# Expert masks by DMA instead of by transpose, two alternating PSUM pairs in the mixed expert blocks, and the second feed-forward beside the first

## The chip, the cores and the metric

The kernel runs on one core of one Trainium2 chip. The metric is the device time of one launch in microseconds, as the median of several runs. A profiled execution gives the trace; its span is the time from the first to the last instruction of the program.

Engine names in the profile: PE is TensorE's matmul, PEld its weight load, DVE is VectorE, ACT is ScalarE, POOL is GpSimd, SP is the queue from which most transfers are issued.

## The reference

One transformer layer in float32 on 4 x 1024 tokens of width 256: a linear-attention block with a feed-forward, and a mixture of experts with low-rank adapters, each inside `x + layernorm(f(layernorm(x)))`. Cut to what matters here:

```python
# attention part, per token block
h = h @ ...                                   # q, k, v, linear attention, wo
x = x + gelu(layernorm(x) @ w_ff1 + b_ff1) @ w_ff2 + b_ff2
x = x @ w_d + b_d

# expert part: D = 256, F = 1024, E = 8 experts, rank R = 16, top K = 2
t = rmsnorm(x) * norm_w
probs = softmax(t @ gate_w.T)
topw, topi = top_k(probs, 2); topw = topw / topw.sum()
base1, base3 = t @ w1.T, t @ w3.T
h1[e] = base1 + 2 * (t @ a1[e].T) @ b1[e].T
h3[e] = base3 + 2 * (t @ a3[e].T) @ b3[e].T
act[e] = silu(h1[e]) * h3[e]
out[e] = act[e] @ w2.T + 2 * (act[e] @ a2[e].T) @ b2[e].T
out = sum over the two chosen experts of weight * out[e]
```

The 8 experts of rank 16 fill 128 partitions together. So the adapters of all experts are one matmul with 128 rows, and a mask of 128 partitions by 512 tokens, 2 where the partition's expert is the token's and 0 elsewhere, keeps the token's own 16 rows.

## The kernel before

**Stages.** The 4096 tokens are eight blocks of 512 (`BLK`), four tiles of 128 (`TB`). `front(i)` makes queries, keys and the context, `middle(i)` the attention's output and the feed-forward in two halves of 256 tokens (`hf`), and `tail(i, hf)` the routing: it sorts each token by its pair of experts and scatters its row of 263 values (`RW`: 256 of x, then the lower and the higher expert `R_LO`, `R_HI`, the weight `R_W`, and others) into the DRAM tensor `rows`. The experts are numbered so that each is in a lower or an upper half (64 partitions each). `ORDER` lists eight expert blocks of 512 rows: four `LU` (one expert in each half; "mixed" below), three `H` (both experts in one half), one `G` (any pair). For each, `prepare(n, ...)` loads the rows and makes masks, weights and the masked adapter inputs, and `experts(n, kind)` does the main work. A branch at the end repeats everything with G blocks when a group has too few places; with this data it isn't taken.

**Order of the work.** The order on TensorE, VectorE, ScalarE and GpSimd is written out by a planner while the program is built. Each stage is a generator wrapped in a `Stream`; a number that it yields is the time at which it wants to go on, a function is a condition. `now()` counts the planned TensorE time; `V`, `A` and `G` book a cost on VectorE, ScalarE and GpSimd; `defer` puts GpSimd work into a list that `catch_up` empties. In the loop at L1578, `side()` picks the first stream of `sides()` that can go on, in the order closing, `prepare_q`, `prepare` (`ready`), tails, fronts, middles (`blocks`) and the rest. Only where no side work can go does the main stream (`experts`) step, and after it a filler from `finals`, the output matmuls of a block. Each engine, and SP too, then works strictly in the order that came out. SP carries the loads of x and z, the stores `kept`, and the loads of `row`.

**prepare, L1011.** L1014 loads the rows (526 KB, in H two loads of 263 KB), three planned microseconds ahead of their use. VectorE compares the expert numbers of a tile with `eidx` (0 to 7, sixteen times each, along the free dimension) into `sel` (L1025 for LU, L1035 for H, L1042 and L1079 for G), which gives the mask with tokens on partitions. `flip` (L299) transposes it on TensorE, four 128x128 tiles to a PSUM tile `pm`, and ScalarE copies it out, times 2, as `m0` (L1057). `weights()` (L1060) does the same for the weight, broadcast over 128 columns: four transposes into `pmw`, then copies into `wt` (L1064) and, by kind, `m1` (L1066 for LU, L1069 and L1070 for H). LU calls it ahead of the token transposes, H and G at the end of `prepare`. There `dm`, the difference of two masks, has been kept in the tile of `wt`. `normed` and `transposed` make the tokens `tT`, and the matmuls `pu` with the adapter inputs times the masks give `u0`.

**LU in experts, L1431 on.** For each of eight f (128 of the 1024 hidden features): `base` makes `ph`, two PSUM banks (for w1 and w3) of one fixed pair `banks(mine)`; ScalarE copies both into the banks `py` (L1449); `halved` adds the low half's adapter to `ph` and the high half's to `py` by matmuls with 64 rows, and applies tanh (L1233) and two VectorE steps each (L1236, L1237); `down_lu` multiplies by `a2`; `mixed` lets GpSimd blend the two activations. `output` (L1333) is the filler: `up` multiplies the blended values by `w2` into the other pair, four matmuls for each f, as soon as GpSimd is through; `finish` adds `b2`. The next LU block may begin its f 0 and f 4 only when the block before has that many of these done (L1442).

**H and G.** `whole_base` alternates the pairs from f to f; `inner` adds the adapters and calls `swiglu` (L1173, L1175, L1176) once for each of the two experts; `rest` (L1378) makes the outputs at the end of a block.

**middle, L755.** L787 lets a block go on to its feed-forward only when that of the block before is through (`fed`); `x1T`, `h2T` and the hidden tiles `g` have one set of buffers.

Of the kernel before, what the change touches and what calls it, by code (L numbers as in the profile page):

```python
# [15 lines left out]
P = 128  # L16
# [37 lines left out]
def sandwich_kernel(  # L54
# [42 lines left out]


# [10 lines left out]
    eidx_b = eidx_f.unsqueeze(1).to_broadcast([P, TB, P])  # L109
    eidx_h = eidx_f.rearrange("p (h r) -> p h r", h=2)  # L110
# [339 lines left out]
    a2_s = wp.tile([P, FC, P], F32, tag="a2_s", name="a2_s")  # L450

    def prepare_ranks():

        yield lambda: once.done
        raw = mp1.tile([P, DC, 2 * P], F32, tag="actB", name="a13_raw")
# [299 lines left out]
    def middle(i):  # L755
# [31 lines left out]
        yield lambda: i == 0 or i - 1 in fed  # L787

        x1T = mp1.tile([P, DC, BLK], F32, tag="copy", name=f"x1T_{i}")
        h2T = blk([P, DC, BLK], "h2T", f"h2T_{i}")  # L790
# [17 lines left out]
        for hf in range(2):  # L808
            ts = slice(hf * W, (hf + 1) * W)
            gs = []  # L810
            for fp in range(FC // 2):
                pf = psum(f"pf_{i}_{hf}_{fp}")
                g = gp.tile([P, BLK], F32, tag="g", name=f"g_{i}_{hf}_{fp}")
# [16 lines left out]
                yield 0.0  # L830
            yield end

            sty, mvy = tiles(f"y_{i}_{hf}", HT)
            for j in range(hf * HT, (hf + 1) * HT):
# [12 lines left out]
                if j % HT < HT - 1:  # L847
                    yield 0.0
# [162 lines left out]
    def prepare(n, kind, src):  # L1011
        row = sp.tile([P, TB, RW], F32, tag="row", name=f"row_{n}")
        for t, ap in src:
            nc.sync.dma_start(out=row[:, t, :], in_=ap)  # L1014
        yield now() + 3.0
        yield lambda: ranked.done
# [4 lines left out]
        sel = m1.rearrange("p (t r) -> p t r", r=P)  # L1021
        if kind == "LU":

            for j in range(TB):
                nc.vector.tensor_tensor(  # L1025
                    sel[:, j, :].rearrange("p (h r) -> p h r", h=2), eidx_h,
                    row[:, j, R_LO : R_HI + 1].unsqueeze(2).to_broadcast([P, 2, HALF]),
                    ALU.is_equal,
                )
                e = V(0.28, 0.0, 1)  # L1030
        elif kind == "H":

            for k in range(2):
                for j in range(2):
                    nc.vector.tensor_tensor(  # L1035
                        sel[:, 2 * k + j, :].rearrange("p (h r) -> p h r", h=2), eidx_h,
                        row[:, j : TB : 2, R_LO + k : R_LO + k + 1].to_broadcast([P, 2, HALF]),
                        ALU.is_equal,
                    )
                    e = V(0.28, 0.0, 1)  # L1040
        else:
            nc.vector.tensor_tensor(  # L1042
                sel, eidx_b, row[:, :, R_LO : R_LO + 1].to_broadcast([P, TB, P]), ALU.is_equal
            )
            e = V(1.1, 0.0, 1)
# [7 lines left out]
        yield e  # L1053
        pm = psum(f"pm_{n}")
        for j in range(TB):
            flip(pm[:, j * P : (j + 1) * P], sel[:, j, :])
        nc.scalar.activation(m0, pm, AF.Copy, scale=SCALING)  # L1057
        e = read_out(A(0.6, now() + 0.2))
        yield 0.0
        def weights():  # L1060
            pm = psum(f"pmw_{n}")
            for j in range(TB):
                flip(pm[:, j * P : (j + 1) * P], row[:, j, R_W : R_W + 1].to_broadcast([P, P]))
            nc.scalar.copy(wt, pm)  # L1064
            if kind == "LU":
                nc.scalar.activation(m1, pm, AF.Identity, bias=flank[:, 1:2], scale=flank[:, 0:1])  # L1066
                A(0.6, now() + 0.2)
            elif kind == "H":
                nc.scalar.copy(m1[0:HALF, 0 : BLK // 2], pm[0:HALF, 0 : BLK // 2])  # L1069
                nc.scalar.copy(m1[HALF:P, 0 : BLK // 2], pm[HALF:P, BLK // 2 : BLK])  # L1070
                A(0.8, now() + 0.2)
            return read_out(A(0.6, now() + 0.2))

        if kind == "LU":
            w = weights()
            defer(("m1", n), w, 1.3, lambda: nc.gpsimd.tensor_tensor(m1, m1, m0, ALU.mult))
            yield 0.0
        if kind == "G":
            nc.vector.tensor_tensor(  # L1079
                sel, eidx_b, row[:, :, R_HI : R_HI + 1].to_broadcast([P, TB, P]), ALU.is_equal  # L1080
            )
            yield V(0.69)
            pm = psum(f"pm1_{n}")
            for j in range(TB):
                flip(pm[:, j * P : (j + 1) * P], sel[:, j, :])
            nc.scalar.activation(m1, pm, AF.Copy, scale=SCALING)
            e = read_out(A(0.6, now() + 0.2))
            yield 0.0

# [6 lines left out]
        yield from transposed(t, f"s{n}", to_t)  # L1096
        us = [u0]
# [9 lines left out]
        elif kind == "H":  # L1107

            dm = wt
# [21 lines left out]
        else:  # L1131
            dm = wt
# [11 lines left out]
        if kind != "LU":  # L1144
            weights()
# [5 lines left out]
    def experts(n, kind):  # L1151
# [71 lines left out]
        def halved(f, ph):  # L1223
# [7 lines left out]
            acts, e = [new(f"act{k}", f"act{k}_{f}") for k in range(2)], []  # L1231
            for act, bank in zip(acts, (ph, py)):
                nc.scalar.activation(act, bank[0], AF.Tanh, scale=0.5)  # L1233
                e.append(A(0.6, at))
# [97 lines left out]

        def output(ahead):  # L1333
            nonlocal po
            yield lambda: ahead is None or ahead.done
            po = banks(1 - mine, f"po_{n}")
            for f in range(FC):
                yield lambda: (n, f, 2) in at_end
# [337 lines left out]
```

## Time and profile before

| what | us |
|---|---|
| median of three runs | 1118.72 (1116.07 to 1121.32) |
| the profiled execution | 1124.33 |
| its span | 1122.6 |
| PE busy | 1060.2 |
| DVE, POOL, ACT busy | 590.8, 393.2, 330.3 |
| first mask transposes (block 0), last (block 7) | at 218.8 and at 1005.2 |
| mixed blocks | some 245 to 778 |
| H blocks, then G | 778 to 1010, then to the end |

The profile page splits the span into 40 slices, of 28 us each; a digit is the busy share in tenths:

```profile
PE   6999999999999999999999999999999999999995
PEld 5777888775576767576676755445767667656444
DVE  5667554746637644835537566453561562463334
ACT  2436333523422432322223313331221230231210
POOL 1011012213323401552413445454561661751742
PEclk9989999999999999999999999999998999999998
DMA  8312601202000200110200101010000100100000
```

A line of the groups view gives line, engine, operation, tiles, shapes and count, then busy time, the mean of one in ns, and the idle time of the engine just before them. A line of the timeline gives start, length, engine, line, operation and count; in brackets the idle time before it and what ended it. Most float32 matmuls show up as two records. A line of the waits view gives who waited for whom: total, times, longest. A line of the DMA view ends with the median time from issue to landing.

### The profile page before, as it was taken

The page shows a single profiled execution, that of the slowest core. Times are in us where ns is not written, and L with a number is a line of the kernel's source. Part 1 is how long each engine was busy: PE and PEld are TensorE (multiplying, and loading weights), DVE is VectorE, ACT ScalarE, POOL GpSimd, SP SyncE. Part 2 cuts the span into 40 slices and gives each one's busy share as a digit, 9 for nine tenths or more (in the row PEclk, how much of TensorE's full clock was granted, in tenths as well). Part 3 has the DMA queues.
Part 4 walks back from the last instruction along what each step waited for, and adds up shares of the span by engine and source line. Part 5 has one row for each costly group of instructions (what it writes and reads, how often), then busy time and mean ns, then how long its engine had stood idle before and what let it go on. Part 6 is the DMA issues. An engine that isn't in the chain of part 4 may idle for free. (4 is left out here: it accounts for less than half of the span.)

```text
span 1122.6 us, 12822 instructions
## 1 busy us (share of the span) xinstructions
PE 1060.2 (94%) x4678; PEld 730.8 (65%) x4678; DVE 590.8 (53%) x1604; ACT 330.3 (29%) x686; POOL 393.2 (35%) x407
## 2 busy tenths in 40 slices
PE   6999999999999999999999999999999999999995
PEld 5777888775576767576676755445767667656444
DVE  5667554746637644835537566453561562463334
ACT  2436333523422432322223313331221230231210
POOL 1011012213323401552413445454561661751742
PEclk9989999999999999999999999999998999999998
DMA  8312601202000200110200101010000100100000
GB/s 270 110 47 66 127 24 34 96 0 77 1 1 1 77 1 0 38 41 0 77 1 1 44 15 58 5 34 1 23 17 0 39 1 1 39 1 1 19 0 22
DMA packets 25428, 39.50 MB, mean 35 GB/s; under 512 B 2704, under 2 KB 19984, under 8 KB 25360
## 3 DMA queue, kind: packets, MB, share of 16 engines
q1 hardware_dynamic: 15296, 23.57, 6.7%
q10 hardware_dynamic: 6992, 6.55, 2.6%
q0 software_dynamic: 3072, 8.51, 2.1%
q8 instruction: 39, 0.64, 0.2%
q14 instruction: 29, 0.24, 0.1%
HBM read 21.50 MB, written 17.12 MB: 34 GB/s over the span
## 5 line engine op out<-in xcount | busy, mean ns | idle before, releaser
L286 PE MATMUL ph<-tT,w_s 128*128 128x256 f32 (+1 forms) x704 | 236.6, 485 | 15.7 <-DVE act L1176 15.1
L286 PEld LDWEIGHTS ph<-tT,w_s 128*128 128x128 f32 x704 | 133.3, 193 | 98.6 <-issue 58.7
L286 PE MATMUL ph<-u,b_s 64*128 64x256 f32 (+2 forms) x576 | 143.9, 464 | 0.6 <-ACT py L1449 0.6
L286 PE MATMUL py<-wff2d,g 128*128 128x264 f32 x512 | 119.2, 386 | 0.0
L286 PE MATMUL pf<-h2T,wff_s 128*128 128x256 f32 x512 | 115.2, 380 | 1.1 <-DVE h2T L802 1.1
L1175 DVE SCALAR_TENSOR_TENSOR act<-act,ph 128x256 f32<-128x256 f32 (+1 forms) x112 | 51.0, 455 | 120.7 <-ACT act L1173 120.5
L286 PEld LDWEIGHTS ph<-u,b_s 64*128 64x128 f32 (+1 forms) x576 | 69.1, 186 | 67.9 <-issue 55.0
L286 PEld LDWEIGHTS pf<-h2T,wff_s 128*128 128x128 f32 x512 | 96.4, 190 | 19.3 <-issue 3.6
L286 PEld LDWEIGHTS py<-wff2d,g 128*128 128x128 f32 x512 | 97.3, 190 | 16.6
L822 ACT ACTIVATE g<-pf,bff 128x256 f32<-128x256 f32 x128 | 52.6, 472 | 113.5 <-PE pf L286 110.0
L1173 ACT ACTIVATE act<-ph 128x256 f32<-128x256 f32 (+1 forms) x112 | 41.3, 412 | 143.9 <-PE ph L286 132.8
L1221 POOL TENSOR_TENSOR actA<-act,act 128x512 f32<-128x512 f32 x32 | 41.2, 1286 | 114.3 <-DVE act L1237 69.9
L1221 POOL TENSOR_TENSOR actB<-act,act 128x512 f32<-128x512 f32 x31 | 40.2, 1296 | 105.6 <-DVE act L1237 52.9
L844 DVE TENSOR_TENSOR x<-py,bd_s 128x264 f32<-128x264 f32 x32 | 13.9, 433 | 119.7 <-PE py L286 119.7
L286 PE MATMUL po<-w_s,actA 128*128 128x256 f32 x256 | 63.9, 387 | 0.9 <-ACT tT L1273 0.9
L324 POOL TENSOR_TENSOR rs_y<-rsa_y,neghalf 128x2 f32<-128x2 f32 x16 | 11.3, 705 | 151.5 <-DVE rsa_y L321 89.6
L286 PE MATMUL py<-u,b_s 64*128 64x512 f32 x128 | 63.4, 615 | 0.0
L286 PE MATMUL po<-w_s,actB 128*128 128x256 f32 x256 | 62.8, 381 | 0.0
L286 PEld LDWEIGHTS po<-w_s,actA 128*128 128x128 f32 x256 | 46.6, 190 | 20.8 <-issue 13.5
L1449 ACT COPY py<-ph 128x512 f32<-128x512 f32 x62 | 34.9, 570 | 80.4 <-PE ph L286 78.1
L286 PEld LDWEIGHTS po<-w_s,actB 128*128 128x128 f32 x256 | 47.5, 190 | 11.9 <-issue 6.4
L1176 DVE TENSOR_TENSOR act<-act,ph 128x256 f32<-128x256 f32 (+1 forms) x112 | 51.4, 459 | 4.9
(266 smaller groups left out, 1692.4 us busy)
## 6 DMA issues: line engine op xcount, KB each, us to landing
rows<-none ACTq DMA_DIRECT2D x4, 1052.0 KB, 11.7
kept<-x SPq DMA_DIRECT2D x8, 526.0 KB, 2.8
x<-in_x_dram SPq DMA_DIRECT2D x8, 512.0 KB, 4.5
w_s<-in_w_dram SPq DMA_DIRECT2D x3, 1024.0 KB, 5.9
z<-in_x_dram SPq DMA_DIRECT2D x6, 512.0 KB, 4.5
row<-rows SPq DMA_DIRECT2D x5, 526.0 KB, 4.1
wff_s<-in_wff_dram SPq DMA_DIRECT2D x2, 1024.0 KB, 9.2
row<-rows SPq DMA_DIRECT2D x6, 263.0 KB, 4.2
```

The costliest lines, as they stand in the source:

```text
L286: nc.tensor.matmul(out_, lhsT=lhsT, rhs=rhs, start=start, stop=stop, **kw)
L324: nc.gpsimd.tensor_tensor(r, a, neghalf[:, 0:n], ALU.pow)
L822: nc.scalar.activation(g[:, k * W : (k + 1) * W], pf[:, k * W : (k + 1) * W], AF.Gelu_apprx_tanh, bias=bff1_s[:, f : f + 1],)
L844: nc.vector.tensor_tensor(y[:, j, :], py[:, 0:DX], bd_s, ALU.add)
L1173: nc.scalar.activation(th, h1, AF.Tanh, scale=0.5)
L1175: nc.vector.scalar_tensor_tensor(th, th, 1.0, h1, ALU.add, ALU.mult)
L1176: nc.vector.tensor_tensor(th, th, h3, ALU.mult)
L1221: lambda x0=x0, x1=x1, op=op: nc.gpsimd.tensor_tensor(ac, x0, x1, op))
L1449: nc.scalar.copy(py[a], ph[a])
```

## The change

Masks and weights are no longer transposed. `eid`, made once, has each partition's expert number. `prepare` copies the three columns `R_LO`, `R_HI`, `R_W` of the block's rows to a line of the new DRAM tensor `lines` (three rows of 512 values), and loads rows of that line back, each broadcast to 64 or 128 partitions (`spread`), all from SP. VectorE then compares the spread expert numbers with `eid` in place. `dm` gets a tile of its own.

```diff
+    lines = dr.tile([NBLK + 1, 3, BLK], F32, tag="lines", name="lines")
...
+        pe_ = psum("peid")
+        flip(pe_[:, 0:P], eidx_f)
+        nc.vector.tensor_copy(eid, pe_[:, 0:1])
...
-        for t, ap in src:
-            nc.sync.dma_start(out=row[:, t, :], in_=ap)
-        yield now() + 3.0
-        yield lambda: ranked.done
+        line = lines[NBLK if n == "all" else n]
+        at = 0
+        for w, ap in src:
+            nc.sync.dma_start(
+                out=row[:, at // P : (at + w) // P, :], in_=ap.rearrange("(t p) d -> p t d", p=P)
+            )
+            nc.sync.dma_start(
+                out=line[:, at : at + w], in_=ap[:, R_LO : R_W + 1].rearrange("n c -> c n")
+            )
+            at += w
...
+        def spread(dst, what, cols=slice(0, BLK)):
+            nc.sync.dma_start(out=dst, in_=line[what, cols].partition_broadcast(dst.shape[0]))
+
+        for h, r in enumerate((slice(0, HALF), slice(HALF, P))):
+            if kind == "LU":
+
+                spread(m0[r, :], h)
+            elif kind == "H":
+
+                for k in range(2):
+                    spread(m0[r, k * HB : (k + 1) * HB], k, slice(h * HB, (h + 1) * HB))
+                spread(m1[r, 0:HB], 2, slice(h * HB, (h + 1) * HB))
+        if kind == "G":
+            spread(m0, 0)
+            spread(m1, 1)
+        spread(wt, 2)
+        landed = now() + 13.0
+        yield now() + 3.0
+        yield lambda: ranked.done
...
         yield from transposed(t, f"s{n}", to_t)
+        yield landed
+        for m in (m0, m1) if kind == "G" else (m0,):
+            nc.vector.tensor_scalar(m, m, eid[:, 0:1], SCALING, ALU.is_equal, ALU.mult)
+            e = V(0.6, 0.0, 1)
+        if kind == "LU":
+            nc.scalar.activation(m1, wt, AF.Identity, bias=flank[:, 1:2], scale=flank[:, 0:1])
+            w = A(0.6)
+            defer(("m1", n), max(e, w), 1.3, lambda: nc.gpsimd.tensor_tensor(m1, m1, m0, ALU.mult))
+        if kind != "LU":
+            dm = mp2.tile([P, BLK], F32, tag="yacc", name=f"dm_{n}")
+        yield 0.0
```

The comparisons into `sel`, the transposes into `pm` and `pmw`, and the copies L1057, L1064, L1069, L1070 and L1086 are gone; L1066 reads `wt` instead of `pmw`.

In the mixed blocks the base alternates between the two pairs once the output of the block before is done. That block's own output waits until its last base is issued, since the other pair is in use until then. The high half goes first through tanh and VectorE where bases alternate, and its copy may start a little earlier:

```diff
-            yield lambda: ahead is None or ahead.done
+            yield lambda: fixed and (ahead is None or ahead.done)
...
-                yield e
+
+                alone = ahead is None or ahead.done
+                if f and alone:
+                    mine = pair[0] = 1 - mine
+                yield free_at[mine]
                 ph = banks(mine, f"ph_{n}_{f}")
                 for a in range(2):
                     base(f, ph, a)
+                    fixed = f == FC - 1
                     if n + f:
                         nc.scalar.copy(py[a], ph[a])
-                        e = A(0.6, max(e1, now() + 0.2))
+                        e = A(0.6, max(e1 - (0.69 if a == 0 else 0.0), now() + 0.2))
...
-                pend, (e, e1) = halved(f, ph)
-                mixed(f, pend, e1)
+                pend, (e, e1) = halved(f, ph, alone)
+                free_at[mine] = e
+                mixed(f, pend, max(e, e1))
```

Block 1 may go on to its feed-forward without block 0's being through, in buffers that the expert blocks use later; block 2 waits for block 0 alone. The steps of the feed-forwards are marked as long, and `side()` takes a long step only where no other side step can go. In `rest` the first two output tiles are made together, f by f:

```diff
-        yield lambda: i == 0 or i - 1 in fed
+        yield lambda: i < 2 or (i - 2 if i == 2 else i - 1) in fed
+        (pool, tag), (pool2, tag2) = (
+            ((mp2, "u0"), (mp2, "tT")) if i == 1 else ((mp1, "copy"), (bp, "h2T"))
+        )
...
+                pool, tag = (mp2, ("yacc", "wt")[fp % 2]) if i == 1 else (gp, "g")
...
-                yield 0.0
-            yield end
+                yield 0.0,
+
+            yield end,
...
-            for j in range(2):
-                for f in range(FC - 1):
-                    if j == 0:
-                        yield lambda: (n, f, 2) in at_end
-                        yield at_end[n, f, 2]
+            for f in range(FC - 1):
+                yield lambda: (n, f, 2) in at_end
+                yield at_end[n, f, 2]
+                for j in range(2):
                     up(j, f)
                     yield 0.0
...
-            return next((s for s in sides() if s.can()), None)
+            can = [s for s in sides() if s.can()]
+            return min(can, key=lambda s: s.long, default=None)
```

## The prediction, made before the changed kernel was built or run

> **What bounds the kernel now.** I read the first part of the page, then the windows of TensorE by stage, its waits, and the timeline around the steps that the change touches.
>
> ```profile
> span 1122.6 us, 12822 instructions
> ...
> PE 1060.2 (94%) x4678; PEld 730.8 (65%) x4678; DVE 590.8 (53%) x1604; ACT 330.3 (29%) x686; POOL 393.2 (35%) x407
> ...
> 78.00:201.00 123.00, 116.59 (x569) 1.00 0.26 62
> ...
> 245.00:700.00 455.00, 440.87 (x1824) 1.00 0.08 27
> 700.00:776.00 76.00, 73.76 (x266) 1.00 0.05 15
> 776.00:1010.00 234.00, 218.89 (x1222) 0.99 0.05 14
> ...
> PE ph L286 <- DVE act L1176: 15.1, 20, 2.8
> ```
>
> TensorE sets the end: of 1122.6 us it is idle 62. The windows give length, busy time, count, granted clock and DMA: the first feed-forwards (78 to 201) leave 6.4 us idle, the mixed blocks (245 to 776) 16.4, the H blocks (776 to 1010) 15.1. The largest single wait, 15.1 us for L1176, is wholly in that last stretch: L1176 belongs to `swiglu`, which only H and G use. The mixed blocks' own waits of that kind (for L1236 and L1449) are 0.6 us each. So what counts is TensorE work removed and idle time in each stretch, not the load of another engine.
>
> **The mask transposes.** 68 are removed: 4 + 4 in each of seven blocks and 12 in G, 17 groups of four.
>
> ```profile
> 566.39 0.60 PE L299 MATMUL pm<-ident,m 128*128 128x128 f32 x4
> 567.55 1.08 PE L286 MATMUL pya<-act,a_s 128*64 128x512 f32 x4 [0.55 <-ACT g L822]
> 568.56 0.70 PE L286 MATMUL po<-w_s,actB 128*128 128x256 f32 x2
> 569.09 0.60 PE L299 MATMUL pmw<-ident,row 128*128 128x128 f32 x4
> 569.53 0.60 PE L299 MATMUL pt_s<-ident,u 128*128 128x128 f32 x4
> ...
> 839.06 0.65 PE L299 MATMUL pmw<-ident,row 128*128 128x128 f32 x4
> 839.64 1.08 PE L286 MATMUL py<-act,a_s 128*64 128x256 f32 x8
> 840.65 1.13 PE L286 MATMUL ph<-u,b_s 64*128 64x256 f32 x8
> 844.58 6.75 PE L286 MATMUL ph<-tT,w_s 128*128 128x256 f32 x16 [2.79 <-DVE act L1176]
> ```
>
> Matmuls overlap, so a group costs the distance to the next start: 0.44 us (569.09 to 569.53) in plain surroundings, 0.58 (839.06 to 839.64) between matmuls on part of the array. Over the 17 groups, 10 at 0.44 and 7 at 0.5 to 0.65, I get 8.4 us (ends: 17 x 0.44 = 7.5, and 10.6, the busy sum of the `pm` and `pmw` groups). TensorE works through nearly all of it, so it comes off the end. The one new transpose for `eid`, with its copy, costs 0.2.
>
> **The weight copies on ScalarE.** In the same place 2.79 us of idle follow, and ScalarE shows why:
>
> ```profile
> 841.98 0.58 ACT L1064 COPY wt<-pmw 128x512 f32<-128x512 f32 x1 [3.99 <-DVE u L1124]
> 842.46 0.36 ACT L1069 COPY m<-pmw 64x256 f32<-64x256 f32 x1
> 842.84 0.37 ACT L1070 COPY m<-pmw 64x256 f32<-64x256 f32 x1
> 843.23 0.66 ACT L1173 ACTIVATE act<-ph 128x256 f32<-128x256 f32 x2
> ```
>
> `dm` and `wt` share a tile, so the copy waits for VectorE's last reading of `dm` (L1124); three copies then stand ahead of the tanh that TensorE needs. The matmul it reads ended at 841.78, so without the copies it starts at 841.85 instead of 843.23: 1.4 us. The same pattern stands at 927; before G the wait is 0.80, of which I take half. Together 3.2 us (ends: nothing, if VectorE is late next, and 7.3, all of 0.9, 2.79, 2.80 and 0.80).
>
> **The clock.** The window 844.5 to 851.4, just after that idle time, has a mean granted clock of 0.55, and 16 matmuls took 6.75 us where they take 3.72 elsewhere: 3.0 lost. After the same 2.80 us at 927 nothing was lost. I credit half, 1.5 (ends: 3.0 gained, 3.0 lost at another gap). The Trainium skill ("TensorE: Matmul & The Clock Gate", "What's actually happening") puts the drop to half rate after an idle window of about 3.4 us; this 2.79 us gap is shorter, and by the rule alone the credit falls and the forecast is 1106.
>
> **The second feed-forward beside the first.** Block 1 no longer waits for block 0 to be through, and steps marked long come after other side work. The work is the same; only the 6.4 us of idle time in its stretch can go. Its longest pieces (1.35 and 0.85 us) wait for VectorE before a feed-forward, which a second block can fill. I take 2 (ends: 0 and 6.4).
>
> **Alternating bases.** The next base no longer waits for the pair that VectorE reads. The rows show that wait already filled: at most two gaps of 0.6 us. The 32 output matmuls (`up`) of a block (0.43 us each, 13.8 us in all) were that filler and now run after the last base; they stay on TensorE. In the last mixed block, where no side work is left, an iteration takes 8.28 us (728.81 to 737.09), of which 1.73 are output matmuls. The rest, 6.55, must hide the chain through `py`: two copies (2 x 0.57), the row matmuls 2.1, a tanh 0.6, two VectorE steps 1.4, about 0.7 of hand-overs, 5.9. It fits by 0.6. I take 0; the ends are 8.2 gained (half of the 16.4) and 5 lost (four iterations at 1.3, should 0.69 of `yacc` and prepare's VectorE work fall into the chain).
>
> **The transfers that take the transposes' place.** Each block now issues on SP the row, a line (three columns of 512 rows, 1536 pieces of 4 bytes, to DRAM), then 3 spreads (7 in H) that wait for the line. VectorE meets them at one place: the mask instruction, which the schedule puts 13 us after the issue where the old comparison stood at 3. Everything later on VectorE stands behind it, and TensorE behind that.
>
> ```profile
> 732.59 0.89 SPq L1014 DMA_DIRECT2D row<-rows  x2
> 738.84 1.58 DVE L1035 TENSOR_TENSOR m<-eidx,row 128x128 f32<-128x128 f32 x2
> 811.71 0.87 SPq L1014 DMA_DIRECT2D row<-rows  x2
> 823.97 1.56 DVE L1035 TENSOR_TENSOR m<-eidx,row 128x128 f32<-128x128 f32 x2
> ...
> b_s<-in_b_dram SPq DMA_DIRECT2D x16, 64.0 KB, 6.3
> ```
>
> Row issue to comparison was 4.7, 8.3, 9.9, 6.2, 6.2, 12.3, 12.2, 12.3 us in blocks 0 to 7; ten more is the room: 14.7, 18.3, 19.9, 16.2, 16.2, 22.3, 22.2, 22.3. No row shows a transfer of 4-byte pieces. In the packet records the smallest data packets (32 bytes) take 9 ns, so 1536 are 0.9 us over 16 DMA engines and 13.8 on one; with 2.6 us, the shortest median landing, the line takes 3.5 to 16.4. The nearest row is the 16-row load above, 6.3; with 0.9 I take 7.2. Chain for LU and G: row issue 0.6, line 7.2, three issues 1.4, last landing 3.7 (a 256 KB load), 12.9. For H: 1.4, 7.2, 3.2 and 3.7, 15.5. Both are inside the room of every block, narrowly in blocks 0 (1.8) and 4 (0.7), so I charge 1 us (ends: 0, and 33 at a line of 16.4, the lateness summed over the blocks). On the SP queue one load follows a row closely, x at 375.94; it would go out some 9 us later, but is first read at 443. The old masks and weights took VectorE 0.9 to 3.1 us and ScalarE 1.2 to 2.0 a block; the new mask instruction, 512 columns, lies between 0.4 (L983, 256 columns) and 0.8, with up to 1.3 of waiting beside GpSimd, and is covered by what it replaces.
>
> The Trainium skill speaks against this line ("DMA: Bandwidth & Descriptors", "Rules for kernel authors"): a strided last dimension makes one descriptor per element, and an outer dimension of three keeps a transfer on three engines. By that rule the pieces take 4.6 us instead of 0.9, an estimate; the line is 10.9, blocks 0, 3 and 4 are late by 5.4 in all, and the forecast would be 1109. No row here shows it.
>
> **Sum.** -8.4 + 0.2 - 3.2 - 1.5 - 2 + 0 + 1 = -13.9 us, on the profiled execution's 1124.33 (span 1122.6): 1110.4. The three other runs have a median of 1118.72, 5.6 lower; the predicted median is 1104.8, say 1105. Its own range is 1096 to 1114, from the ends above, most of which won't meet.
>
> **Rivals.** (1) *The line is slow.* At 16.4 us the blocks are late by 7.4, 3.8, 2.2, 5.9, 8.5, 2.4, 2.5 and 0, 32.7 in all, on VectorE's queue and so on TensorE: 1118.7 - 14.9 + 32.7 = 1136. It decides for slower from a line of about 13.7 us, where the lateness reaches 15. For it: 1536 pieces, unlike any transfer in the trace, and the comparison already waited for the row in block 0. Against: 10 us of added room, and DMA engines idle (0.05 busy after 245). (2) *Gains given back.* The transposes go, but the ends fall badly elsewhere: 5 lost in the last mixed block, no clock credit, no gain from the feed-forwards: -8.2 - 3.2 + 5 + 1 = -5.4, 1113; with the weight copies' gain lost as well 1116. For it: small waits after reordering come from durations that the schedule misjudges. (3) *The mixed blocks' idle time goes too*, half of 16.4: 1097. Against: those waits are for routing and for attention (L913, L907, L709), which the change doesn't touch. That the transfers bring a transpose back under another name is excluded by the diff.
>
> **Numbers.** Forecast 0.60, (1) 0.16, (2) 0.17, (3) 0.07. A measurement of this kernel tells 0.5%, 5.6 us, from no change. The forecast and (3) are faster, (2) mostly within: faster 0.70, same 0.13, slower 0.17. The range 1096 to 1123 leaves out most of (1) and little below.
>
> **What would show it.** No `pm` or `pmw` groups, TensorE's busy time down by 8 to 12; the wait for L1176 under 12 us, its two long gaps near 1.4; the line landing under 12 us and VectorE not waiting for spreads by more than 1 us. Wrong it would be with VectorE waiting for `m0` for several us in blocks 0, 3 and 4, or with new waits for the `py` copies in the last mixed block.

## The result, and the profile after

The change made the kernel slower by a tenth: 1234.67 us (1233.78 to 1236.55), beside 1118.81 for the kernel before on the same chip; the ratio is 1.1038, with a 95% interval of 1.1009 to 1.1067. The profiled execution has a span of 1233.0 us, 110.4 more than before.

The first part of the page after, with busy time of each engine, share of the span and instructions:

```profile
span 1233.0 us, 12714 instructions
...
PE 1053.9 (85%) x4611; PEld 723.9 (59%) x4611; DVE 575.6 (47%) x1584; ACT 319.2 (26%) x663; POOL 391.8 (32%) x407
```

TensorE's work fell by 6.3 us (1060.2 to 1053.9); its idle time grew from 62 to 179. The windows of the kernel after say where (length, then busy time and count of PE, PEld, DVE, ACT and POOL, then granted clock, DMA share and GB/s):

```profile
78.00:201.00 123.00, 115.62 (x569) 96.92 (x568) 72.74 (x269) 48.55 (x102) 18.63 (x24) 1.00 0.24 62
245.00:700.00 455.00, 418.49 (x1694) 281.65 (x1693) 233.17 (x702) 129.84 (x261) 142.91 (x138) 0.97 0.12 26
700.00:800.00 100.00, 19.22 (x62) 7.05 (x60) 7.40 (x12) 5.59 (x10) 14.06 (x12) 0.61 0.44 14
...
874.00:1110.00 236.00, 224.01 (x1255) 165.09 (x1254) 111.83 (x261) 52.37 (x132) 116.97 (x100) 1.00 0.07 22
```

From 700 to 800 TensorE works 19 us of 100: it stands still ahead of block 3. From 245 to 700 it is idle for 36.5 us, where it was for 14.1. The last row, the H blocks, is no worse than before. TensorE's waits after (line waited for, total, times, longest):

```profile
PE pt_s L299 <- DVE u L995: 85.0, 1, 85.0
PE ph L286 <- DVE act L1160: 13.4, 21, 1.4
PE pf L286 <- DVE u L1092: 13.2, 1, 13.2
PE pctx L286 <- ACT mix L715: 10.1, 1, 10.1
PE pctx L286 <- DVE u L1092: 9.2, 1, 9.2
...
PE ph L286 <- ACT py L1440: 4.4, 2, 2.2
```

The second row is the old wait for L1176, now L1160. Four waits are new and large: 85.0 + 13.2 + 10.1 + 9.2 = 117.5. Three stand behind VectorE, and the fourth (10.1) behind ScalarE, so the waits of these two for DMA are read next:

```profile
DVE u L995 <- DMA row<-rows: 89.2, 1, 89.2
DVE m L1076 <- DMA m<-lines: 45.5, 3, 15.6
...
ACT m L1079 <- DMA wt<-lines: 45.6, 3, 19.7
```

There are two causes. VectorE waits once, 89.2 us, for the *rows* of block 3, and three times, 45.5 us, for the *spreads* of blocks 0 to 2 at the mask instruction L1076; TensorE covers some 13 of the 45.5. ScalarE waits in the same places for the spread of the weights. The SP queue's timeline shows both; first block 0:

```profile
209.23 0.61 SPq L1028 DMA_DIRECT2D row<-rows  x1
209.90 0.87 SPq L1031 DMA_DIRECT2D lines<-rows  x1
236.52 1.16 SPq L1042 DMA_DIRECT2D m<-lines  x2
```

The spreads go out as soon as the line is there, 26.6 us after its issue; in blocks 1 and 2 after 26.7 and 27.8. Priced were 7.2, at most 16.4. Then the same queue ahead of block 3:

```profile
676.55 54.04 SPq L1031 DMA_DIRECT2D lines<-rows  x5
730.70 11.83 SPq L1042 DMA_DIRECT2D m<-lines  x2
742.63 0.53 SPq L1042 DMA_DIRECT2D wt<-lines  x1
743.21 2.37 SPq L1042 DMA_DIRECT2D m<-lines  x4
751.15 19.13 SPq L1031 DMA_DIRECT2D lines<-rows  x3
770.39 19.28 SPq L1028 DMA_DIRECT2D row<-rows  x1
```

Eight lines, all that are left (blocks 3 to 7), are issued in one bunch *ahead of* block 3's row, although `prepare` writes each block's row before its line. With earlier lines under way, five of these eight issues take 10.8 to 16.6 us and the row's own takes 19.3, the other three 0.7 to 2.4. The row goes out at 770.39, 94 us after the first line of the bunch. So the account of SP in the kernel's description was wrong: the written order holds for the four engines that `tc.manual_schedule` names (L1520 of the kernel before), and SP isn't among them.

### The profile page after: what moved, and what is told of

It reads as the page before. It is cut to its first block, busy times and chain, and to the rows that moved or that the text cites. A ratio compares the mean times of both kernels' runs of the same rounds, so it can differ in the third digit from the quotient of the medians.

```text
span 1233.0 us, 12714 instructions
## 1 busy us (share of the span) xinstructions
PE 1053.9 (85%) x4611; PEld 723.9 (59%) x4611; DVE 575.6 (47%) x1584; ACT 319.2 (26%) x663; POOL 391.8 (32%) x407
## 5 line engine op out<-in xcount | busy, mean ns | idle before, releaser
L286 PE MATMUL ph<-tT,w_s 128*128 128x256 f32 (+1 forms) x704 | 235.6, 483 | 13.4 <-DVE act L1160 13.4
L286 PE MATMUL ph<-u,b_s 64*128 64x256 f32 (+2 forms) x576 | 146.4, 469 | 4.4 <-ACT py L1440 4.4
L286 PE MATMUL pf<-h2T,wff_s 128*128 128x256 f32 x512 | 120.2, 390 | 14.8 <-DVE u L1092 13.2
L286 PEld LDWEIGHTS py<-wff2d,g 128*128 128x128 f32 x512 | 97.3, 190 | 16.6
L299 PE MATMUL pt_s<-ident,u 128*128 128x128 f32 x64 | 9.7, 294 | 85.0 <-DVE u L995 85.0
L286 PE MATMUL py<-u,b_s 64*128 64x512 f32 x128 | 66.1, 638 | 0.0
L299 PEld LDWEIGHTS pt_s<-ident,u 128*128 128x128 f32 x64 | 7.9, 149 | 88.3 <-issue 85.8
```

What stands on the lines that cost most here:

```text
L286: nc.tensor.matmul(out_, lhsT=lhsT, rhs=rhs, start=start, stop=stop, **kw)
L299: nc.tensor.transpose(out_, in_, ident)
```

## The experiments

Two theories to start from. O: the SP order is the cause. L: the line is, however SP is ordered. All ratios are to the kernel before on the same chip, with their 95% interval.

| kernel | median us | ratio | interval |
|---|---|---|---|
| the change | 1234.67 | 1.1038 | 1.1009 to 1.1067 |
| sp_order | 1177.71 | 1.0529 | 1.0512 to 1.0547 |
| sp_order_32 | 1135.37 | 1.0130 | 1.0101 to 1.0159 |
| masks_only | 1264.82 | 1.1299 | 1.1280 to 1.1318 |
| masks_sp32 | 1137.24 | 1.0177 | 1.0153 to 1.0201 |
| jump | 1131.74 | 1.0096 | 1.0059 to 1.0133 |
| jump_alone_sp | 1127.70 | 1.0057 | 1.0025 to 1.0089 |
| one_flip | 1121.43 | 1.0022 | 0.9997 to 1.0048 |
| one_flip_alone | 1114.82 | 0.9958 | 0.9943 to 0.9974 |
| alt_only | 1123.00 | 1.0049 | 1.0035 to 1.0063 |
| alt_ff | 1121.09 | 1.0025 | 1.0006 to 1.0045 |
| ff_only | 1114.48 | 0.9955 | 0.9927 to 0.9983 |
| ff_one_flip | 1116.27 | 0.9981 | 0.9952 to 1.0010 |
| ff_cols | 1109.82 | 0.9934 | 0.9910 to 0.9957 |
| cols_alone | 1124.70 | 1.0046 | 1.0029 to 1.0063 |
| cols_all | 1107.94 | 0.9902 | 0.9869 to 0.9936 |

**Which fault.** The whole change with SP in the written order:

```diff
-    with tc.manual_schedule(engines={EN.PE, EN.DVE, EN.Activation, EN.Pool}):
+    with tc.manual_schedule(engines={EN.PE, EN.DVE, EN.Activation, EN.Pool, EN.SP}):
```

> The changed kernel (1234.7), with the SP queue too kept in the order in which the program text issues its transfers. Theory O (order): 85 us of the loss is one wait, because SP issued the lines of blocks 3 to 7 in one bunch ahead of block 3's row; in program order this goes, and what is left are the late masks of the separate blocks: 1140 to 1165, with no single TensorE wait over 20 us. Rival L (the line's own time): some 27 us from issue to landing against the 13 that the schedule allows is the cause everywhere, so blocks 3 to 7 now pay 10 to 15 us each as blocks 0 to 2 do: 1195 to 1215.

1.0529, 1177.71 us, lies between the ranges of O and L: half of the loss goes with the order. The 85 us wait is gone, and the spreads are now late in every block, as VectorE's waits in this run say:

```profile
DVE m L1076 <- DMA m<-lines: 72.1, 9, 16.1
```

With this on top, the schedule knows how slow the line is:

```diff
-        landed = now() + 13.0
+        landed = now() + 32.0
```

> As sp_order, and the mask instruction is scheduled 32 us after the issue instead of 13. If the rest of the loss is only that VectorE stands at the mask instruction while the line is under way, those waits go and the time is 1105 to 1118, at or below before (1118.8): the gains of the forecast show at last. If the late mask instead delays the blocks' start, mostly in H and G where nothing else is left to do, TensorE idles there for 10 us or more per block and the time stays at 1140 or above.

VectorE no longer waits for spreads; it waits for rows (27.7 us in 4). Three of the four waits are for the second half of an H block's rows, which stands on the queue behind the slow line of the first half. 1.0130 lies between the two expectations: told the truth, the schedule still can't hide the line.

**Which part.** Alternating bases and feed-forward without the masks (`alt_ff`), and the masks alone (`masks_only`), each with the diff's own code, cut here to a line of each:

```diff
+                if f and alone:
+                    mine = pair[0] = 1 - mine
...
+        yield lambda: i < 2 or (i - 2 if i == 2 else i - 1) in fed
```

```diff
+            nc.vector.tensor_scalar(m, m, eid[:, 0:1], SCALING, ALU.is_equal, ALU.mult)
```

> The kernel before with the alternating bases and the second feed-forward beside the first, and with the old masks by transposes. My forecast for these two parts was -2 us: 1112 to 1119. Rival: the last mixed block without its filler, and the reordering, cost 5 or more: 1122 to 1130. If the loss of the whole change had a part here, it would be well above that.

> The kernel before with the masks by transfers alone. Theory: the whole loss is in this part, 1220 to 1245, with lines of later blocks again ahead of a row on SP. Rival: it takes the alternating bases (whose outputs come later and so hold the row's buffer longer) for the bunching to hurt: then 1150 to 1190 here.

1.0025 and 1.1299: but for some 3 us the loss is the masks', and alone they lose more than was expected. TensorE's first wait in `masks_only` is for block 3's row again, and the queue shows the same bunch, from 715.81 to the row at 811.23.

```profile
PE pt_s L299 <- DVE u L989: 103.3, 1, 103.3
```

The masks alone with SP ordered and 32 us allowed come near `sp_order_32`, at 1.0177:

> The kernel before with the masks by transfers as in the change, SP in program order and the mask instruction scheduled after 32 us. Measured so far 1264.8 for the masks alone and 1135.4 for the whole change with these two repairs. Theory: the two repairs take away nearly all of the loss here too: 1120 to 1140. If SP's bunching and the early mask are not the whole cause: above 1160.

**Masks without the line's transfer.** In these two, one transpose for each block comes back: VectorE gathers the three columns into 12, one transpose and one copy turn them, and one store of 12 x 512 bytes makes the line (SP ordered). The mask instruction is planned 8 us after that store, 10 in H.

```diff
-            nc.sync.dma_start(
-                out=line[:, at : at + w], in_=ap[:, R_LO : R_W + 1].rearrange("n c -> c n")
-            )
...
+        nc.vector.tensor_copy(cols, row[:, :, R_LO : R_W + 1].rearrange("p t c -> p c t"))
+        nc.tensor.transpose(pl[0 : 3 * TB, 0:P], m1[:, P : P + 3 * TB], ident)
+        nc.scalar.copy(lt, pl[0 : 3 * TB, 0:P])
+        nc.sync.dma_start(out=line.rearrange("c (t p) -> (c t) p", p=P), in_=lt)
```

> The changed kernel with SP in program order, and the line made otherwise: VectorE gathers the three columns of the block's rows into 12 columns, one transpose on TensorE turns them into 12 rows of 128, ScalarE copies them out, and one transfer stores them as 12 pieces of 512 bytes. The spreads and the masks stay. Theory: the 1536 pieces of 4 bytes are what makes the line take 27 us; with 12 pieces the store lands within 3 us, the spreads within 8 of it, VectorE waits for spreads under 3 us in all, and the gains of the forecast show: 1103 to 1114. Rival: the spreads (broadcast reads of one DRAM row by 64 or 128 partitions) are slow as well, and the masks are again late: 1125 or more.

> The same line by one transpose in the kernel before, without alternating bases and without the second feed-forward beside the first, SP in program order. Theory: like one_flip within 5 us (1105 to 1116), since those two parts measured +2 us together. If it is faster than one_flip by 3 or more, those parts cost time here too.

1.0022 for the whole change so mended, 0.9958 for the masks alone; 1103 to 1114 was expected of the first, which measured 1121.43. VectorE has no wait for spreads left. So spreading the masks from DRAM is cheap; making the line was the cost.

**What makes the line slow.** Copies that nothing reads were added to the kernel before, beside the row loads. The first set varied the size of the pieces and where they come from and go to:

```diff
+                nc.sync.dma_start(out=lines[n], in_=three.rearrange("n c -> c n"))
...
+                nc.sync.dma_start(out=triples, in_=three)
...
+                nc.sync.dma_start(out=lt, in_=three.rearrange("n c -> c n"))
...
+                    nc.sync.dma_start(
+                        out=lines[n][c].rearrange("(t p) -> p t", p=P), in_=row[:, :, R_LO + c]
+                    )
```

> The kernel before, with copies on SP that nobody reads: after block 0's row the three columns as 1536 pieces of 4 bytes, DRAM to DRAM, as in the change; after block 1's the same columns as 512 pieces of 12 bytes; after block 2's the columns from the row tile in SBUF to DRAM, 1536 pieces in three transfers; after block 3's as 1536 pieces from DRAM into three SBUF partitions. If the number of pieces sets the time (some 17 ns each, whatever the number of DMA engines): 26, 9, 26 and 26 us. If writes of 4 bytes to DRAM set it: the last one, into SBUF, is under 10 us. If DMA engines do: the third is some 1 to 5 us and the last the longest.

By the packet records (time in which all but the first and last 2% of the pieces began) the same transfer took 16.2 us, 512 pieces of 12 bytes 0.7, 1536 pieces of 4 bytes from SBUF in three transfers 1.4, and 1536 pieces into SBUF 4.4. So neither 1536 pieces nor 4-byte writes to DRAM are slow as such. The next guess (theory W) was that writes side by side are, so the pieces were laid 512 bytes apart:

```diff
-            nc.sync.dma_start(
-                out=line[:, at : at + w], in_=ap[:, R_LO : R_W + 1].rearrange("n c -> c n")
-            )
+            for c in range(3):
+                nc.sync.dma_start(
+                    out=line[c, at : at + w].rearrange("(t j) -> j t", j=P),
+                    in_=ap[:, R_LO + c].rearrange("(t j) -> j t", j=P),
+                )
```

> The changed kernel, SP's order untouched, with one edit: the line is copied column by column in an order in which pieces that follow each other land 512 bytes apart instead of side by side (three transfers of 512 pieces for one of 1536; in H six of 256 for two of 768). Theory W: 4-byte pieces written one behind the other into the same stretch of DRAM are what takes 27 us, so this line lands in 3 to 6 us. Then blocks 0 to 2 no longer wait (32 us back), and what is left of the 85 us wait is the time to issue the bunch ahead of block 3's row, some 25 transfers at 0.6 us: 1125 to 1145. Rival S: copies from DRAM to DRAM in pieces of 4 bytes are slow in any order: 1200 or more.

> The kernel before with the masks by transfers alone, the line in the jumping order, SP in program order, the mask instruction still 13 us after the issue. By W: the chain of row, line and spreads is 10 to 13 us and the masks wait little: 1108 to 1122. By S: as sp_order, 1170 or more.

> The kernel before, with copies on SP that nobody reads. After block 0's row: the three columns DRAM to DRAM in the jumping order. After block 1's: from the row tile in SBUF to DRAM so that 16 pieces in a row go side by side. After block 2's: DRAM to DRAM side by side again, but one transfer for each column. After block 3's: as in the change. By W the first takes 3 to 6 us, the second clearly longer than the 3 us that SBUF to DRAM took in the jumping order, the third and fourth some 20 to 27. By S the first takes 20 or more and the second 3.

The line became fast (in blocks 0 to 2 of `jump` the spreads go out 9.6 to 10.0 us after the line's issue), and the change's ratio 1.0096 with SP's order still free: the bunch is issued in 645 to 687, and block 3's row costs VectorE a wait of 21.4 us, not 89. `jump_alone_sp`, at 1127.70, came out above its 1108 to 1122. And W fell: `probe2` moved the pieces in under 1 us side by side too, as long as each transfer held one column. What was left, many pieces in a transfer or the form of the access, `probe3` told apart.

```diff
+                nc.sync.dma_start(out=column, in_=rows[0 : 3 * BLK, R_LO])
...
+                nc.sync.dma_start(
+                    out=lines[n][:, 0:P], in_=three[0:P, :].rearrange("n c -> c n")
+                )
...
+                nc.sync.dma_start(out=lines[n][1:3, :], in_=three[:, 1:3].rearrange("n c -> c n"))
...
+                nc.sync.dma_start(out=lines[n].rearrange("c n -> n c"), in_=three)
```

> Unread copies in before, beside the row loads of blocks 0 to 3. Block 0: one column of 1536 rows in one transfer (1536 pieces). Block 1: three columns of 128 rows in one transfer (384 pieces). Block 2: one column of 512 rows, then two columns. Block 3: three columns of 512 rows, walked row by row, written column by column. Theory N (many pieces in one transfer are slow): block 0 takes 15 us or more, block 1 under 5, block 3 15 or more. Theory A (three columns in one transfer, laid on few DMA engines or walked badly, are slow): block 0 under 5 us, block 1 a quarter of 18, block 2's second copy about 12 and its first 2 or less, block 3 either way.

The records of the 4-byte pieces on SP's queue (time as above; most under way at once), and, from the semaphore records of the same traces, how many completion signals each transfer got after its issue (where there are fewer than 16, one more comes as the issue ends):

| transfer | pieces | time us | at once | signals |
|---|---|---|---|---|
| the change, block 0: 3 columns of 512, column by column | 1536 | 16.0 | 8 | 3 |
| the same, `probe2` | 1536 | 17.0 | 9 | 3 |
| one column in each of 3 transfers, `probe2` | 3 x 512 | 0.6 | 31 | 16 each |
| one column of 1536, `probe3` | 1536 | 0.9 | 28 | 16 |
| 3 columns of 128, column by column, `probe3` | 384 | 0.8 | 8 | 3 |
| one column of 512, then 2 columns in one, `probe3` | 512 + 1024 | 16.6 | 21 | 16, then 2 |
| 3 columns of 512, row by row, `probe3` | 1536 | 0.6 | 30 | 16 |
| 3 columns of 512, column by column, into SBUF, `probe` | 1536 | 4.4 | 7 | 3 |

All but the last go from DRAM to DRAM.

Theory N fell (1536 pieces in one transfer took 0.9). What is left of A is the walk, not its numbers: it expected a quarter of 18 us for 128 rows (0.8 measured) and about 12 for two columns (16.6). Slow, from DRAM to DRAM with 512 rows, is the walk whose outer step is 2 or 3 columns. Such transfers have at most 8 or 9 pieces under way where the others have 28 to 31 (the 21 are those of the one column that went first), and two columns take as long as three, as if each column went its own way. The page "DMA: Bandwidth & Descriptors" of the Trainium skill ("Why a DMA increments its semaphore by 16 and not by 1") says that the number of engines is the largest up to 16 that divides the slowest dimension of both sides: 3 for three columns walked column by column, 2 for two, 16 for the rest. The engine of a packet isn't recorded, but the signals in the last column are just these numbers, and the line of `one_flip`, stored as 12 rows, has 12.

Few engines alone don't make a transfer slow, though. Into SBUF 1536 pieces with 3 signals took 4.4 us, and 384 pieces took 0.8. In the slow transfers some pieces stall: of the 1571 4-byte records around block 0's line, 184 took 0.1 to 2.2 us each, 76 of the 90 us that all took together, where none of the fast transfers, nor the one into SBUF, has a record of 0.1 us. Why they stall, and why not among the first, stays open: of the change's 1536 pieces, the first 37% passed in 1.6 us and the other 970 took 14.3.

**The other parts.** Feed-forward and the order of long steps alone, and alternating bases alone, of the first diff above the third line and the first two:

> The kernel before with the second feed-forward beside the first and the long steps last, nothing else. Both parts together measured 1.0025 of before. My forecast for this part alone was -2 us (1113 to 1118) and 0 for the bases. Rival: it is this part that costs, by the new order of the side work: 1120 to 1126, and the bases are worth 0 or a gain.

> The alternating bases alone on before. If their cost is what the differences of the other runs say (alt_ff less ff_only, one_flip less one_flip_alone, both near 7 us): 1124 to 1128, with two new waits near 2.2 us for the py copies in the last mixed block and the rest spread over the mixed blocks. If the cost only arises beside the other parts: 1117 to 1121.

0.9955 and 1.0049. `alt_only` has one of the two 2.2 us waits for the `py` copies that it was to show. Its timeline (start, duration) tells what is late:

```profile
726.78 1.26 POOL L1221 TENSOR_TENSOR actA<-act,act 128x512 f32<-128x512 f32 x1 [2.73 <-DVE lm_o L1299]
726.81 1.25 DVE L1302 TENSOR_TENSOR lm_o<-lm_o,row 128x4 f32<-128x4 f32 x1
727.53 1.08 PE L286 MATMUL pya<-act,a_s 128*64 128x512 f32 x4
...
728.18 2.08 ACT L1306 ACTIVATE tT<-tT,lm_o,rs_o 128x256 f32<-128x256 f32 x4 [3.89 <-DVE lm_o L1302]
...
730.17 1.05 ACT L1456 COPY py<-ph 128x512 f32<-128x512 f32 x2
...
730.79 0.69 PE L286 MATMUL ph<-u,b_s 64*128 64x512 f32 x1 [2.18 <-ACT py L1456]
```

A four-element VectorE step (0.17 at 477 and 622 in this trace) takes 1.25 us beside a GpSimd step that begins and ends with it; ScalarE waits for it, then runs four copies of another block's `end` (2.08), and only then the two `py` copies. The next 7 us (731 to 738) have a granted clock of 0.76. The Trainium skill ("TensorE: Matmul & The Clock Gate", "What's actually happening") ties the drop to about 3.4 us of idle time; here 2.18 us were enough. It doesn't always come: of two such waits of 2.18 us in `cols_all` below, the one ending at 666.4 is followed by a low clock (0.57 from 666 to 670), the one ending at 742.7 by none (1.00 from 742 to 749).

**Putting it together.** Masks by the diff's own line, but one column to a transfer, SP ordered; first with the feed-forward and without alternating bases (beside it the one-transpose form), then the whole change, then the masks alone:

```diff
+            for c in range(3):
+                nc.sync.dma_start(out=line[c, at : at + w], in_=ap[:, R_LO + c])
```

> Before, with the second feed-forward beside the first (and long steps last) and with the masks from spreads, the line made by one transpose and stored once, SP in the written order; without the alternating bases. If the parts add up: one_flip_alone gave 0.9958, ff_only 0.9955, together 0.991, 1109 (1106 to 1113), with TensorE busy 1054 and its idle time at or under 62 us. If the two share their gain (both fill the same idle time before block 1 is through), 1113 to 1116. If alternating bases were needed to reach the gain of the whole, it would be above one_flip's 1121.

> The same, but with the change's own line from DRAM to DRAM, written as three transfers of one column each (512 pieces of 4 bytes) instead of one transfer of three columns (1536), no transpose. Theory T (the single three-column transfer is what took 18 to 27 us; one column at a time takes about 2): the spreads go out some 6 us after the row, no wait of VectorE for them over 3 us in all, and the time is that of ff_one_flip less up to 3 us: 1105 to 1113. Rival (pieces of 4 bytes are slow wherever the kernel's other transfers run beside them): the spreads go out 15 us or more after the row, VectorE waits 20 us or more, 1125 or above.

> The whole change with its two faults mended and nothing else touched: the line as three transfers of one column each, SP in the written order. If line and order are all that made it slower, and the alternating bases cost what alt_only showed (5.5) on top of ff_cols (0.9934): 0.998 to 1.000, 1115 to 1119, without a wait for spreads over 3 us, with the 2.2 us waits for the py copies in the last mixed block. If the three parts disturb one another beyond that, 1122 or above. If the prediction's sum was right once the line is fast (alternating bases at nothing): 1105 to 1110.

> The masks by transfers alone, with the column-wise line and SP in the written order. The prediction's terms for the masks (-8.4, +0.2, -3.2, -1.5, +1) are -11.9 or 0.989, 1106. one_flip_alone, with a transpose and a copy more for each block and its line stored from SBUF, gave 0.9958; ff_cols less the gain of ff_only (0.9955) would be 0.998. If masks and feed-forward are each worth what they were alone, 1110 to 1115; if they share idle time, down to 1108.

`ff_one_flip` gave 0.9981, 1116.27 us, where 1106 to 1113 was expected if the parts add up: they don't. In `ff_cols`, 0.9934, SP issues block 0's spreads 8.9 us after the line:

```profile
206.81 0.61 SPq L1028 DMA_DIRECT2D row<-rows  x1
207.47 1.90 SPq L1032 DMA_DIRECT2D lines<-rows  x3
216.32 0.47 SPq L1041 DMA_DIRECT2D m<-lines  x1
```

`cols_all`, the whole change with its two faults mended, is the fastest in median, 1107.94 or 0.9902, and beats the kernel before. Expected was 1115 to 1119, or 1105 to 1110 if alternating bases cost nothing. Its TensorE waits, in its profiled execution (1117.77 at a mean granted clock of 0.984, the slowest of its six; the fastest is 1101.94 at 0.996):

```profile
PE ph L286 <- DVE act L1159: 13.4, 21, 1.4
PE pcg L286 <- DVE gate_s L402: 8.7, 1, 8.7
PE ph L286 <- ACT py L1439: 4.4, 2, 2.2
```

No compute engine's waits in this profile name a spread or a block's rows. With line and order mended nothing else was touched and nothing of the loss is left, so the two faults are all of it. `cols_alone` was a miss: 1.0046, where at most 1115 was expected. In its profile the mixed blocks (245 to 776) are idle for 27.8 us, 16.4 before, with waits of 5.1, 3.5 and 3.2 us for VectorE that the kernel before doesn't have; why they arise is not shown. Alone, masks (+5.1), feed-forward (-5.0) and alternating bases (+5.5) sum to +5.6 us of 1119; together they give -11.0. Parts of a planned order need not add; that each changes which work fills which gap is the likely reason, not a shown one.

## Why the prediction was wrong, by its own steps

**The step that failed** is "The transfers that take the transposes' place", charged at 1 us; the measured loss around it is 117.5 us of TensorE waits. It failed twice.

The *line's price*: 7.2 us, ends 3.5 to 16.4, measured 26.6 to the first spread's issue, of which the pieces took 16.0 and some 7 passed after the last. The 9 ns of a packet row was multiplied by 1536 on one engine and called the upper end. It was read from 32-byte packets of another transfer; here it is the median piece, and the 184 pieces that took 0.1 us or more set the slow line apart. No row showed them, so 16.4 was no bound. The rule that it quoted gave three engines, as the three signals do, and the 10.9 made from it failed by the same 9 ns. Rival (1), "The line is slow", had the right mechanism at a chance of 0.16, with its price cut off at that bound. By its sum a line of 26.6 costs over 100 us; with SP in order the loss was 59 (`sp_order`), since only part of each lateness reaches TensorE.

The *queue*: "On the SP queue one load follows a row closely" looked at who stood behind the row in the old order. The change puts transfers on a queue whose order nobody fixes, so the question was also what may be put ahead of the row. L1520 names four engines, and SP isn't one of them. With fast lines the free order still cost a 17.2 us wait of TensorE for block 3 (`jump`); with slow ones 85.0.

The other steps:

- *Mask transposes, -8.4*: TensorE's busy time fell by 6.3 in the kernel after, and by 4.3 in the profile of `cols_all`, below the 8 to 12 that were to show it; a slower clock in that profile (0.98 in 245 to 700, against 1.00) may hide part of it. The `pm` and `pmw` groups are gone.
- *Weight copies, -3.2*: the two gaps of 2.8 became at most 1.4, as said, and the wait for L1176 went from 15.1 to 13.4, not under 12. Right mechanism, size nearer 2. In `one_flip_alone` the covering work failed in the way that the lower end named: the mask instruction takes 1.50 us beside GpSimd (0.48 at 396.5; 0.4 to 0.8 plus 1.3 were allowed) and `dm` 1.37, and VectorE is late next:

```profile
832.55 1.50 DVE L1078 TENSOR_SCALAR m<-m,eid 128x512 f32<-128x512 f32 x1
...
834.09 1.37 DVE L1099 TENSOR_TENSOR dm<-m 128x256 f32<-128x256 f32 x1
...
837.50 2.93 PE L286 MATMUL ph<-tT,w_s 128*128 128x256 f32 x6 [2.60 <-DVE act L1162]
```

- *Clock, -1.5*: in 776 to 860 the mean granted clock was 0.96 before and is 1.00 in `cols_all`. Right in sign there; over the whole span that profile has 0.984, before 0.988, so as a gain of the whole it isn't shown.
- *Feed-forward, -2*: -5.0 alone (1.9 to 8.2), but not where it was looked for. In `ff_only` 78 to 201 is idle 7.5 us (6.4 before), and 245 to 700, in the mixed blocks, 9.7 (14.1 before). Right in sign, not in its reason.
- *Alternating bases, 0 with an end of +5*: +5.5 alone (3.9 to 7.0). The chain through `py` was said to fit by 0.6 us; it was counted without ScalarE's work of another block's `end`, which stands ahead of the copies. In `alt_only` the wait of 2.2 and the slow 7 us after it (24% of 7, 1.7) are 3.9 of the 5.5; beside the feed-forward (`alt_ff`) there are two such waits, and the difference to `ff_only` is 7. Beside the mended masks the cost isn't seen: `cols_all` and `ff_cols` have intervals that overlap. What alternation is worth there stays open.

With both faults mended the whole measures 1104.6 to 1112.1 by its interval, with the 1105 forecast at its lower end. That is in good part luck and doesn't vindicate the terms: the masks alone lost 5 us in this form (and gained 4.7 with one transpose, `one_flip_alone`) where the terms gave -11.9, and the feed-forward alone gained 5 where they gave 2.

## What to carry to other kernels

Before a transfer gets a price, write out how it is walked on both sides: if the outer step is 2 or 3 and there are hundreds of small pieces for each, as here from DRAM to DRAM, suspect it, and split it by column or turn the walk around. Before transfers are put on a queue, see whether its order is fixed, and ask what may land ahead of the one that the next stage needs. And an upper end made of rows of another kind of transfer is no bound: probe it, or leave the range open on that side.

## What was not expected of the hardware

- DRAM to DRAM, transfers of equal bytes and equal pieces (1536 of 4 bytes) took from 0.6 to 17 us, by the walk alone; the slow walk, into SBUF, took 4.4.
- The transfers walked in 2, 3 or 12 outer steps got just as many completion signals after their issue, the other forms tried here 16.
- Seven issues on SP took 10.8 to 19.3 us while earlier slow transfers were under way (676 to 790), against 0.4 to 2.4 for the others in that stretch, and held up whatever stood behind them.
- VectorE steps beside GpSimd: 1.50 us for 512 columns (0.48 elsewhere), and 1.25 for four (0.17 elsewhere).
